# One core, attention and routed experts: heads of the first sequence scaled on GpSimd, 32-bit counts in the searches, and new places for every step

## The chip, the core and the metric

The kernel runs on one core of a Trainium2 chip. The metric is device time in microseconds (us), the median of several executions. TensorE does the matmuls (PE in the profile; PEld is its weight load, which runs beside matmuls), VectorE is DVE, ScalarE is ACT, GpSimd is POOL and SyncE is SP. All work together through semaphores, each in the order in which its instructions are written.

## The reference

`x` has 16 sequences of 256 tokens of 256 channels, all in 32-bit floats.

```
shift = silu(t) @ W_ada.T + b_ada
h = layernorm(x) * g + b + shift
q, k, v = split(h @ Wqkv.T)                 # 16 heads of 64 channels
q, k = layernorm of each head (gain, bias)
x = x + concat(softmax(q k^T / 8) v) @ Wout.T
tok = x.reshape(4096, 256)
gate = softmax(tok @ Wgate.T)               # 8 experts
vals, idx = top_k(gate.T, 512)              # each expert takes its 512 best tokens
g = layernorm(tok[idx])
y = (gelu(g @ fc1.T + b1) @ fc2.T + b2) * vals
tok[idx] += y                               # a token may be taken by several experts
```

## The kernel before

**Attention.** Each sequence is two tiles of 128 tokens. `First` normalises the tokens, transposes them and adds the shift. A `Group` is one of six blocks of 512 columns of the qkv product on one token tile: groups 0 and 1 are q, 2 and 3 are k, 4 and 5 are v. Its matmul (L611) puts 128x512 numbers into PSUM under the tag "mm", which has three buffers. For v, ACT copies them out (L620). For q and k the mean has been taken out of the weights beforehand (`center`, L531 to L533), so that a head's norm needs the squares (ACT, L624), their sum (DVE, L628 and L632), the power -1/2 (POOL, L82), the multiplication (`scale`, L644), four transposes on PE (L653), and an eviction with gain and bias (ACT, L665). `scale` reads PSUM on DVE, unless `keep` has had ACT copy the block to SBUF (L606); then it runs on POOL. In the kernel before only the last sequence has places for `keep`.

A `Quad` is four heads. Scores (L686) are matmuls on half the rows of the array, maxima are on DVE (L693), exponentials on ACT (L702), normalising on POOL (L713), transposes on PE (L722) with copies on DVE or ACT (L730, L732), and the product with v (L740) is on half the columns. `Tail` projects (L764), adds the residual, normalises for the experts and computes gate logits (L797, a 32-bit product of eight columns).

**Routing.** A first routing covers the first 15 sequences' 30 tiles; a second covers all 32 tiles and leaves out what the first has taken. Each picks 256 tokens for every expert by a search over the bits of the threshold: 30 steps, from bit 29 down. A step compares all gates with the candidate and sums the hits of each partition (DVE, L881, into `cnt`), adds these over the 16 partitions of each expert by a matmul with a block matrix, and decides the bit. In the first search (`count_over`) the count comes with a constant taken off, so that its sign decides:

```
nc.tensor.matmul(self.pc, ones[:1, :P], less, start=True, stop=False)
nc.tensor.matmul(self.pc, twice, self.cnt, start=False, stop=True)
```

These are L911 and L912, both in bf16. Meanwhile `either` computes both candidates of the next step (L918, two instructions), and `decide` picks one by a maximum and a minimum (L927). The second search has one count matmul in a step (`count`, L888, with `block`), then `drop` (L893) and `step` (L900).

**Experts.** A job is one expert in one routing: 16 jobs. Onehots (L1031) and their product (L1040) turn places into a list of tokens; `take` makes indices and weights; `gather` fetches the rows by two indirect DMAs from POOL's queue (L1059); transposes (L1068) and an eviction (L1075) follow, then `up` (L1087), gelu (L1094), `down` (L1103), `finish` (L1109, L1110), and `scatter` (L1113), which adds the rows to the output by an indirect DMA from POOL, one for each half of 128 tokens.

**Order.** The order of the instructions is written out by hand. Each step of the attention, of the first routing and of the first jobs has a place number: `STEADY` for a sequence, shifted by its number times `PERIOD`, with `START` in its stead for the first sequences and `END` for the last, and tables for gates, search, lists, `UP` and `DOWN`. `at` collects steps with their places, and all are issued in the order of the numbers. The first search is thus mixed with the attention of the last sequence. The later jobs come from a loop of 16 slots for each job, in which the list and gather of the next job stand at slot 5 and its transposes at slot 14; the second search's steps are dealt out over the slots. Job 0's scatters have places, in the table `DOWN`:

```
at(DOWN[i][1:], partial(jobs[0].scatter, i))
```

**Loads.** SP loads the first sequence, qkv groups 4, 0 and 2 and, each some time ahead, the sequences from the third on. ACT's queue loads the second sequence, groups 1, 3 and 5 and the output weights `wo`, at one place (`LOADS`).

Of the kernel before, what the change touches and what calls it, by code (L numbers as in the profile page):

```python
# [43 lines left out]
def kernel(  # L44
# [35 lines left out]
    def rsqrt(dst, src):  # L80
# [14 lines left out]
    twice = const.tile([P, P], BF16, name="twice")  # L95
    nc.gpsimd.tensor_scalar(twice, block, 2.0, None, ALU.mult)
    less = const.tile([1, 1], BF16, name="less")
    nc.gpsimd.memset(less, -2.0 * (CAP // 2 - 1))
# [30 lines left out]
    nc.gpsimd.memset(gate_of, -1.0)  # L129
    high = const.tile([P, 1], I32, name="high")  # L130
# [9 lines left out]
    PERIOD = 55.238  # L140
    STEADY = dict(
        first=((-88.131, -77.795, -66.865), (-86.413, -85.278, -65.341), (-64.291, -63.624)),
        group={
            (0, 0): (-49.424, -47.476, -46.806, -45.766, -41.767, -39.325, -32.822),
            (0, 1): (-38.888, -36.940, -36.270, -35.230, -33.490, -28.967, -28.300),
            (1, 0): (-19.721, -16.746, -15.194, -14.154, -10.700, -4.932, -1.947),
            (1, 1): (-21.934, -19.241, -18.571, -17.531, -15.791, -5.369, -4.702),
            (2, 0): (-37.170, -35.222, -34.552, -33.512, -31.772, -26.157, -20.051),
            (2, 1): (-27.875, -25.927, -25.257, -24.217, -21.020, -13.051, -9.617),
            (3, 0): (-2.777, -0.829, 1.424, 2.464, 6.338, 15.371, 16.143),  # L150
            (3, 1): (-4.495, -2.547, -1.877, -0.837, 4.102, 8.406, 9.073),
            (4, 0): (-52.511, -43.423),
            (4, 1): (-31.559, -29.611),
            (5, 0): (-16.692, -14.744),
            (5, 1): (-8.179, -6.231),
        },
        quad={
            (0, 0): (0.000, 6.254, 13.508),
            (0, 0, 0): (2.224, 4.501, 6.524, 8.843, 9.510),
            (0, 0, 1): (2.821, 3.601, 7.430, 9.280, 9.947),  # L160
            (0, 1): (-1.059, 4.018, 13.509),
            (0, 1, 0): (0.230, 1.010, 4.288, 7.969, 10.110),
            (0, 1, 1): (0.827, 1.910, 5.194, 7.532, 8.362),
            (1, 0): (11.585, 16.798, 31.441),
            (1, 0, 0): (14.068, 14.848, 17.068, 25.834, 28.523),
            (1, 0, 1): (12.874, 13.654, 17.974, 23.242, 26.227),
            (1, 1): (12.644, 23.095, 31.442),
            (1, 1, 0): (16.201, 20.616, 24.292, 26.708, 27.923),
            (1, 1, 1): (14.665, 21.516, 23.386, 25.397, 27.748),
            (2, 0): (29.518, 34.134, 56.102),  # L170
            (2, 0, 0): (30.807, 31.587, 35.310, 37.672, 38.339),
            (2, 0, 1): (31.404, 32.487, 34.404, 37.235, 37.902),
            (2, 1): (30.577, 35.467, 56.103),
            (2, 1, 0): (32.598, 33.387, 39.367, 46.622, 49.992),
            (2, 1, 1): (32.001, 34.287, 36.216, 38.109, 39.092),
            (3, 0): (40.264, 45.901, 64.955),
            (3, 0, 0): (43.941, 44.721, 46.171, 48.777, 50.676),
            (3, 0, 1): (41.553, 42.333, 47.077, 49.432, 51.346),
            (3, 1): (41.323, 50.592, 64.956),
            (3, 1, 0): (43.014, 43.794, 51.768, 60.225, 60.892),  # L180
            (3, 1, 1): (42.417, 47.782, 50.862, 59.788, 60.639),
        },
        out=(15.601, 33.534, 58.656, 67.053),
        tail=((75.024, 80.051, 81.151, 92.875, 82.383, 82.831, 90.365, 92.705), (97.967, 101.653, 107.912, 115.175, 104.452, 104.900, 115.900, 117.411)),
# [3 lines left out]
            first=((-139.487, -139.084, -130.002), (-134.729, -123.135, -95.026), (-71.635, -61.204)),  # L188
            group={
                (0, 0): (-59.500, -57.180, -53.990, -41.905, -41.892, -31.199, -19.864),  # L190
                (0, 1): (-56.514, -46.937, -42.187, -36.541, -32.975, -14.723, -12.430),
                (1, 0): (-11.345, -10.160, -10.123, -9.363, -7.717, 16.862, 17.870),
                (1, 1): (-17.061, -12.458, -10.932, -9.433, -9.429, -7.544, -7.063),
                (2, 0): (-47.944, -39.268, -37.967, -29.426, -29.083, -19.329, -15.473),
                (2, 1): (-36.593, -35.280, -31.121, -27.896, -26.496, -20.716, -17.116),
                (3, 0): (-0.195, 1.354, 5.032, 6.866, 7.484, 18.359, 20.756),
                (3, 1): (-7.052, -4.047, -4.021, -2.780, 5.168, 9.583, 16.657),
                (4, 0): (-61.161, -56.511),
                (4, 1): (-24.033, -19.174),
                (5, 0): (8.030, 14.550),  # L200
                (5, 1): (-0.065, 4.397),
            },
            quad={
                (0, 0): (-9.254, 22.590, 42.649),
                (0, 0, 0): (-4.098, 3.192, 35.521, 40.175, 42.160),
                (0, 0, 1): (-7.788, -2.839, 22.830, 27.700, 30.119),
                (0, 1): (-10.825, 1.530, 42.650),
                (0, 1, 0): (-9.045, -8.059, 15.256, 16.378, 17.222),
                (0, 1, 1): (-6.921, -0.152, 15.562, 17.096, 23.635),
                (1, 0): (0.126, 14.031, 62.413),  # L210
                (1, 0, 0): (5.581, 9.438, 28.540, 45.916, 48.521),
                (1, 0, 1): (6.615, 11.701, 34.709, 42.123, 45.511),
                (1, 1): (6.647, 32.947, 62.414),
                (1, 1, 0): (12.684, 22.346, 38.667, 41.778, 42.977),
                (1, 1, 1): (16.709, 24.888, 35.995, 40.496, 41.536),
                (2, 0): (36.613, 44.084, 79.640),
                (2, 0, 0): (38.678, 40.096, 53.301, 75.810, 75.857),
                (2, 0, 1): (37.844, 41.179, 46.653, 73.800, 78.092),
                (2, 1): (31.788, 44.810, 79.641),
                (2, 1, 0): (35.309, 35.316, 47.104, 63.762, 75.398),  # L220
                (2, 1, 1): (35.999, 36.383, 45.887, 51.730, 53.463),
                (3, 0): (57.532, 66.273, 80.859),
                (3, 0, 0): (62.041, 62.092, 75.830, 76.948, 78.262),
                (3, 0, 1): (58.897, 62.045, 71.274, 78.272, 80.335),
                (3, 1): (42.288, 56.582, 80.861),
                (3, 1, 0): (53.169, 56.538, 74.699, 79.614, 79.641),
                (3, 1, 1): (55.287, 56.039, 56.589, 75.724, 78.348),
            },
            out=(52.169, 77.187, 79.720, 81.968),
            tail=((83.431, 83.938, 98.840, 128.374, 103.780, 103.911, 108.593, 110.466), (101.110, 104.350, 128.872, 145.215, 106.950, 107.929, 158.941, 161.116)),  # L230
        ),
        1: dict(
            first=((-46.775, -2.928, 1.521), (-17.063, -5.314, 0.982), (15.343, 17.672)),
            group={
                (0, 0): (18.719, 22.736, 28.212, 28.786, 33.289, 38.005, 45.577),
                (0, 1): (21.654, 25.091, 29.577, 30.657, 37.616, 45.616, 50.362),
                (1, 0): (56.965, 58.830, 59.835, 62.211, 62.315, 70.246, 74.608),
                (1, 1): (56.747, 57.357, 58.840, 58.862, 61.374, 62.457, 62.468),
                (2, 0): (40.127, 40.864, 42.252, 42.262, 45.473, 48.208, 52.717),
                (2, 1): (40.977, 41.918, 42.391, 45.462, 46.160, 49.170, 52.410),  # L240
                (3, 0): (74.826, 75.081, 75.503, 78.958, 80.988, 81.454, 84.690),
                (3, 1): (72.447, 74.612, 74.727, 79.840, 80.430, 81.825, 83.328),
                (4, 0): (36.938, 40.518),
                (4, 1): (52.802, 53.597),
                (5, 0): (63.613, 73.243),
                (5, 1): (30.152, 33.881),
            },
            quad={
                (0, 0): (80.434, 81.692, 98.968),
                (0, 0, 0): (80.662, 81.021, 85.076, 94.133, 94.171),  # L250
                (0, 0, 1): (80.458, 80.463, 87.029, 93.291, 94.064),
                (0, 1): (58.862, 78.602, 98.969),
                (0, 1, 0): (66.341, 68.024, 80.857, 85.468, 86.358),
                (0, 1, 1): (68.231, 73.899, 80.721, 81.679, 85.268),
                (1, 0): (80.676, 90.848, 105.478),
                (1, 0, 0): (81.477, 86.038, 92.163, 96.097, 96.147),
                (1, 0, 1): (82.096, 83.656, 93.097, 94.720, 94.811),
                (1, 1): (88.704, 93.176, 105.479),
# [1067 lines left out]
```

## Time and profile before

| | |
|---|---|
| median of 3 executions | 1194.63 us (1194.6 to 1195.56) |
| the profiled execution | 1194.45 us |
| its span | 1192.6 us |
| mean granted clock of TensorE | 0.992 |
| PE busy | 1162.9 us, 98% |
| PEld busy | 817.1 us, 69% |
| DVE busy | 760.9 us, 64% |
| ACT busy | 624.5 us, 52% |
| POOL busy | 590.7 us, 50% |

A group of instructions in the profile shows line, engine, operation, output and input tiles with their shapes and their number, then busy time in all, mean ns of one, and the engine's idle time just before them with what ended it. A wait shows the waiting instruction, what it waited for, and the total in us, how often, and the longest. The granted clock is the share of full speed that the throttle allowed. Line numbers are those of the kernel before.

### The profile page before, as it was taken

The page shows a single profiled execution, that of the slowest core. Times are in us where ns is not written, and L with a number is a line of the kernel's source. Part 1 is how long each engine was busy: PE and PEld are TensorE (multiplying, and loading weights), DVE is VectorE, ACT ScalarE, POOL GpSimd, SP SyncE. Part 2 cuts the span into 40 slices and gives each one's busy share as a digit, 9 for nine tenths or more (in the row PEclk, how much of TensorE's full clock was granted, in tenths as well). Part 3 has the DMA queues.
Part 4 walks back from the last instruction along what each step waited for, and adds up shares of the span by engine and source line. Part 5 has one row for each costly group of instructions (what it writes and reads, how often), then busy time and mean ns, then how long its engine had stood idle before and what let it go on. Part 6 is the DMA issues. An engine that isn't in the chain of part 4 may idle for free. (4 is left out here: it accounts for less than half of the span.)

```text
span 1192.6 us, 19612 instructions
## 1 busy us (share of the span) xinstructions
PE 1162.9 (98%) x6814; PEld 817.1 (69%) x6814; DVE 760.9 (64%) x2274; ACT 624.5 (52%) x1701; POOL 590.7 (50%) x820
## 2 busy tenths in 40 slices
PE   7999999999999999999999999999998989999996
PEld 3566666666676666666666666667755878888885
DVE  7665576666566666666666666565588557865541
ACT  2765655565565656565656566556574422333331
POOL 4665455545555555555554555464674233333332
PEclk9999999999999999999999999999999999999999
DMA  5000000000000000000000000000200446666661
GB/s 187 1 1 5 14 18 19 10 18 10 19 23 5 23 10 19 10 23 6 23 10 28 9 11 14 14 19 19 85 9 1 168 129 186 186 186 185 183 185 22
DMA packets 46738, 62.40 MB, mean 52 GB/s; under 512 B 3888, under 2 KB 39984, under 8 KB 46640
## 3 DMA queue, kind: packets, MB, share of 16 engines
q1 hardware_dynamic: 37680, 49.82, 12.3%
q0 software_dynamic: 6144, 8.39, 3.8%
q10 hardware_dynamic: 2816, 2.95, 0.7%
q8 instruction: 54, 0.88, 0.3%
q14 instruction: 44, 0.36, 0.1%
HBM read 48.56 MB, written 12.58 MB: 51 GB/s over the span
## 5 line engine op out<-in xcount | busy, mean ns | idle before, releaser
L611 PE MATMUL pm<-wq,hT 128*128 128x512 f32 x768 | 365.3, 606 | 2.2 <-ACT qT L665 0.9
L713 POOL TENSOR_SCALAR pr<-pr,sums 128x256 f32<-128x256 f32 x512 | 236.8, 481 | 208.9 <-DVE sums L709 162.2
L82 POOL TENSOR_TENSOR ss<-ss,neghalf 128x8 f32<-128x8 f32 x128 | 211.5, 1653 | 189.8 <-DVE ss L632 185.4
L702 ACT ACTIVATE pr<-sc,nmax 128x256 f32<-128x256 f32 x512 | 236.1, 474 | 116.1 <-DVE nmax L693 111.1
L611 PEld LDWEIGHTS pm<-wq,hT 128*128 128x128 f32 x768 | 134.9, 192 | 126.3 <-issue 112.2
L693 DVE TENSOR_REDUCE nmax<-sc 128x2 f32<-128x512 f32 x256 | 166.5, 683 | 38.3 <-PE sc L686 38.1
L628 DVE TENSOR_REDUCE ss<-sq 128x8 f32<-128x512 f32 x128 | 87.3, 682 | 112.0 <-ACT sq L624 111.5
L722 PEld LDWEIGHTS pp<-ident,pr 128*128 128x128 f32 x1024 | 119.1, 142 | 43.6 <-POOL pr L713 20.3
L722 PE MATMUL pp<-ident,pr 128*128 128x128 f32 x1024 | 139.2, 273 | 0.2
L624 ACT ACTIVATE sq<-pm 128x512 f32<-128x512 f32 x128 | 76.7, 600 | 113.6 <-PE pm L611 107.1
L686 PE MATMUL sc<-kT,qT 64*128 64x256 f32 x1024 | 129.2, 390 | 0.0
L740 PE MATMUL po<-prT,v 128*64 128x256 f32 x1024 | 126.7, 389 | 0.0
L686 PEld LDWEIGHTS sc<-kT,qT 64*128 64x128 f32 x1024 | 93.2, 186 | 40.6 <-issue 30.4
L1103 PE MATMUL py<-w,hid 128*128 128x256 f32 x512 | 118.8, 385 | 0.0
L1087 PE MATMUL ph<-xT,w 128*128 128x256 f32 x512 | 118.4, 384 | 0.0
L764 PE MATMUL pw<-wo,oT 128*128 128x256 f32 x512 | 118.0, 384 | 0.0
L1113 POOL DMA_INDIRECT out<-y,idx x32 | 51.6, 1611 | 123.9 <-DVE y L1110 72.9
L764 PEld LDWEIGHTS pw<-wo,oT 128*128 128x128 f32 x512 | 96.8, 192 | 18.9 <-issue 6.5
L1094 ACT ACTIVATE hid<-ph,vec 128x256 f32<-128x256 f32 x128 | 60.3, 473 | 85.5 <-PE ph L1087 73.4
L1103 PEld LDWEIGHTS py<-w,hid 128*128 128x128 f32 x512 | 95.8, 192 | 13.4
L702 ACT ACTIVATION_READ_ACCUMULATOR pr<-sc,nmax 128x1 f32 x512 | 104.9, 205 | 0.0
L1087 PEld LDWEIGHTS ph<-xT,w 128*128 128x128 f32 x512 | 95.3, 191 | 13.4
(129 smaller groups left out, 1290.7 us busy)
## 6 DMA issues: line engine op xcount, KB each, us to landing
w<-in_fc2T SPq DMA_DIRECT2D x16, 1024.0 KB, 5.6
w<-in_fc1T SPq DMA_DIRECT2D x16, 1024.0 KB, 8.0
out<-tok SPq DMA_DIRECT2D x32, 128.0 KB, 1.7
xn_dram<-tn SPq DMA_DIRECT2D x32, 128.0 KB, 1.7
xs<-in_x SPq DMA_DIRECT2D x15, 256.0 KB, 2.7
b<-in_b2s SPq DMA_DIRECT2D x16, 128.0 KB, 8.2
wq<-in_wqkvT SPq DMA_DIRECT2D x3, 512.0 KB, 6.6
wq<-in_wqkvT ACTq DMA_DIRECT2D x3, 512.0 KB, 6.6
```

Source lines behind the costliest of these rows:

```text
L82: nc.gpsimd.tensor_tensor(dst, src, neghalf[:, : src.shape[1]], ALU.pow)
L611: nc.tensor.matmul(self.pm, hTs[self.b][:, c, bass.ts(self.t, P)], wq[:, c, bass.ts(self.g, GW)], start=(c == 0), stop=(c == DC - 1),)
L628: nc.vector.tensor_reduce(self.ss[:, 0, :], self.sq.rearrange("p (h d) -> p h d", d=HD), AX.X, ALU.add,)
L686: nc.tensor.matmul(self.sc[i, j][:, t, :], qTs[self.b][rows, hp, bass.ts(t, P)], kTs[self.b][rows, hp, :], start=True, stop=True,)
L693: nc.vector.tensor_reduce(self.nmax[i, j], self.sc[i, j], AX.X, ALU.max, negate=True)
L702: nc.scalar.activation(self.pr[i, j][:, t, :], self.sc[i, j][:, t, :], AF.Exp, bias=self.nmax[i, j][:, t : t + 1], scale=1.0, accum_out=se ...
L713: nc.gpsimd.tensor_scalar(self.pr[i, j][:, t, :], self.pr[i, j][:, t, :], self.sums[i][:, 1, j, t : t + 1], 1.0, ALU.mult, ALU.mult,)
L722: nc.tensor.transpose(self.pp[i, j][:, c, bass.ts(t, P)], self.pr[i, j][:, t, bass.ts(c, P)], ident,)
L740: nc.tensor.matmul(self.po[j * HD : (j + 1) * HD, i, :], vs[self.b][:, c, bass.ts(4 * self.d + 2 * i + j, HD)], self.prT[i, j][:, c, :], s ...
L764: nc.tensor.matmul(self.pw, oTs[self.b][:, hp, bass.ts(self.t, P)], wo[:, hp, :], start=(hp == 0), stop=(hp == HP - 1),)
L1087: nc.tensor.matmul(self.ph[f], self.w1[:, c, bass.ts(f, P)], self.xT[:, c, :], start=(c == 0), stop=(c == DC - 1),)
L1103: nc.tensor.matmul(self.py[i], self.hid[:, f, bass.ts(i, P)], self.w2[:, f, :], start=(f == 0), stop=(f == FC - 1),)
```

## The change

- **Counts in 32 bits.** `cnt` becomes a 32-bit float, `blockf` is a 32-bit copy of `block`, and `twice` is a 32-bit float. The second search counts with `blockf`. In the first, the comparison starts its sum on each partition at -(256-1)/16, and the one-row matmul with the constant goes.
- **Candidates from a table.** `change` holds, for each bit, the two words with which the candidate is XORed; `either` becomes one instruction. Five small DVE instructions fill the table at place 4.5 periods, and POOL prepares its exponents.
- **First sequence.** Its eight q and k groups get a place for `keep`: ACT copies them out of PSUM, and POOL scales them.
- **Loads.** ACT's queue takes the second sequence and qkv groups 5, 1 and 3 at one place, and the third sequence, `wo`, the fourth and the fifth at a second one. SP loads the sequences from the sixth on.
- **Job 0's scatters.** Only the half that ends first has a place; the other is issued behind job 2's gather.
- **New places** for every step, and `PERIOD` 55.497 in place of 55.238.

```diff
+    blockf = const.tile([P, P], F32, name="blockf")
+    nc.gpsimd.tensor_copy(blockf, block)
+    twice = const.tile([P, P], F32, name="twice")
     nc.gpsimd.tensor_scalar(twice, block, 2.0, None, ALU.mult)
-    less = const.tile([1, 1], BF16, name="less")
-    nc.gpsimd.memset(less, -2.0 * (CAP // 2 - 1))
...
+    change = const.tile([P, 30, 2], I32, name="change")
+    powers = const.tile([P, 31], I32, name="powers")
+    nc.gpsimd.iota(powers, pattern=[[1, 31]], base=126, channel_multiplier=0)
+
+    def fill_change():
+        nc.vector.tensor_scalar(powers, powers, 23, None, ALU.logical_shift_left)
+        nc.vector.tensor_copy(change[:, :, 0], powers[:, :30].bitcast(F32))
+        nc.vector.tensor_tensor(
+            change[:, :, 1], powers[:, :30].bitcast(F32), powers[:, 1:].bitcast(F32), ALU.add
+        )
+        for k in range(2):
+            nc.vector.memset(change[:, 0, k : k + 1], k)
...
-    PERIOD = 55.238
+    PERIOD = 55.497
...
     START = {
         0: dict(
...
-                (0, 0): (-59.500, -57.180, -53.990, -41.905, -41.892, -31.199, -19.864),
+                (0, 0): (-73.721, -55.814, -49.484, -45.811, -35.989, -25.285, -20.864, -40.370),
...
         def later_loads():
             load_x(1, nc.scalar)
-            for g in (1, 3, 5):
+            for g in (5, 1, 3):
                 load_wq(g, nc.scalar)
+
+        def last_loads():
+            load_x(2, nc.scalar)
             nc.scalar.dma_start(wo, woutT.rearrange("(h p) d -> p h d", p=P))
+            for b in (3, 4):
+                load_x(b, nc.scalar)
...
-            def compare(self, n):
+            def compare(self, n, begin=0.0):
                 reach = bit.tile([P, 2 * P], BF16, tag="reach", name="reach")
-                self.cnt = bit.tile([P, 1], BF16, tag="cnt", name="cnt")
+                self.cnt = bit.tile([P, 1], F32, tag="cnt", name="cnt")
                 nc.vector.tensor_scalar(
-                    reach, self.gT, self.cand.bitcast(F32), None, ALU.is_ge, ALU.add,
+                    reach, self.gT, self.cand.bitcast(F32), begin or None, ALU.is_ge, ALU.add,
                     accum_out=self.cnt,
                 )
...
-                nc.tensor.matmul(self.pc, block, self.cnt, start=True, stop=True)
+                nc.tensor.matmul(self.pc, blockf, self.cnt, start=True, stop=True)
...
+            def compare_less(self, n):
+
+                self.compare(n, -(CAPL - 1) / 16)
+
             def count_over(self, n):
...
-                nc.tensor.matmul(self.pc, ones[:1, :P], less, start=True, stop=False)
-                nc.tensor.matmul(self.pc, twice, self.cnt, start=False, stop=True)
+                nc.tensor.matmul(self.pc, twice, self.cnt, start=True, stop=True)
 
             def either(self, n):
-                self.next = []
-                for name, op in (("keep", ALU.bitwise_or), ("drop", ALU.bitwise_xor)):
-                    new = bit.tile([P, 1], I32, tag=name, name=name)
-                    nc.vector.tensor_scalar(
-                        new, self.cand, 0 if name == "keep" else 1 << n, (1 << n) >> 1,
-                        op, ALU.bitwise_or,
-                    )
-                    self.next.append(new)
+                self.next = bit.tile([P, 2], I32, tag="next", name="next")
+                nc.vector.tensor_tensor(
+                    self.next, self.cand.to_broadcast([P, 2]), change[:, n, :], ALU.bitwise_xor
+                )
...
-            if b > 1:
+            if b > 4:
                 at([min(its["first"][t][0] for t in range(TB)) - 20.0], partial(load_x, b))
...
+        at([4.5 * PERIOD], fill_change)
...
-            at(DOWN[i][1:], partial(jobs[0].scatter, i))
+        by_end = sorted(range(KL), key=lambda i: DOWN[i])
+        at(DOWN[by_end[0]][1:], partial(jobs[0].scatter, by_end[0]))
...
                     new.gather()
+                    if k == 1:
+                        jobs[0].scatter(by_end[1])
```

The other lines of the diff are the tables of places.

## The prediction

> **What bounds the kernel now.** The profiled execution took 1194.45 us, its span 1192.6, so 1.85 us lie outside; the median, 1194.63, is 0.18 us above it. The sum below goes by the profiled time. I read the page's first part (PE busy 1162.9 us, 98%), then the windows by stage, PE's waits, the groups, and the timeline where the windows show holes.
>
> ```profile
> 0.00:20.00 20.00, 13.47 (x31) 6.68 (x32) 13.82 (x34) 4.80 (x8) 9.26 (x24) 1.00 0.82 278
> 20.00:40.00 20.00, 17.55 (x64) 8.52 (x62) 16.23 (x36) 11.43 (x27) 9.06 (x7) 0.91 0.01 2
> 255.20:310.50 55.30, 55.30 (x320) 36.78 (x319) 35.80 (x83) 32.60 (x95) 29.78 (x45) 1.00 0.05 15
> 850.00:900.00 50.00, 47.23 (x276) 30.05 (x274) 39.73 (x164) 29.46 (x82) 31.37 (x45) 1.00 0.17 56
> 900.00:950.00 50.00, 45.30 (x293) 35.02 (x290) 36.22 (x176) 17.94 (x42) 18.39 (x30) 0.93 0.21 70
> 950.00:1000.00 50.00, 46.55 (x300) 39.47 (x299) 30.83 (x161) 15.71 (x32) 17.47 (x18) 0.97 0.56 164
> ```
>
> Columns: stretch, length, busy time of PE, PEld, DVE, ACT, POOL, then granted clock and DMA. A steady sequence (third line) has PE busy throughout: only PE work counts there. Holes lie at the start, around the first search (867 to 909 us) and until job 2's gather (965 us). The clock column counts too: 0.91 over 20 us is 3.6 us at half rate, 0.93 and 0.97 over 50 us are 7 and 3.
>
> ```profile
> PE pa L499 <- ACT sT L494: 5.1, 1, 5.1
> PE pc L912 <- DVE reach L881: 4.0, 14, 0.5
> PE px L1068 <- DMA xg<-xn_dram,idx: 3.8, 3, 2.6
> POOL out L1113 <- DMA out<-y,idx: 6.9, 1, 6.9
> ```
>
> The first wait is before the first matmul and is not touched. The other three are what the edits aim at.
>
> ```profile
> L644 DVE TENSOR_TENSOR qk<-pm,ss 128x512 f32<-128x512 f32 x120 | 81.3, 678 | 9.3 <-POOL ss L82 9.0
> L644 POOL TENSOR_TENSOR qk<-qk,ss 128x512 f32<-128x512 f32 x8 | 8.4, 1065 | 0.1
> L82 POOL TENSOR_TENSOR ss<-ss,neghalf 128x8 f32<-128x8 f32 x128 | 211.5, 1653 | 189.8 <-DVE ss L632 185.4
> L606 ACT COPY qk<-pm 128x512 f32<-128x512 f32 x8 | 4.6, 594 | 0.2 <-PE pq L653 0.2
> L911 PE MATMUL pc<-less,ones 1*128 1x1 bf16 x30 | 5.2, 172 | 0.0
> L912 PE MATMUL pc<-cnt,twice 128*128 128x1 bf16 x30 | 5.1, 170 | 4.3 <-DVE reach L881 4.0 <-ACT prT L732 0.3
> ```
>
> The eight POOL scales are the last sequence's; they price the first sequence's.
>
> **Part 1, the start: -4.0 us.** PE's spacing here against its steady spacing (429 ns per pass of L611, 109 per transpose) gives 5.6 us lost between 17 and 27 us: waits of 1.2, 1.8 and 1.1 at 17.6, 20.2 and 22.4, the rest in the half-rate stretch 23.4 to 26.9. Each wait is for a DVE scale or ACT's eviction behind it: a pm buffer is held through square 0.60, reduce 0.68+0.18, power 1.65 and scale 0.68. With the ACT copy it is free after square and copy, 1.2 us, and DVE loses 8 x 0.68 = 5.4 us of work. ACT gains 8 x 0.59 = 4.7 us; it was 11.43 of 20 us busy. POOL gains 8 x 1.065 = 8.5 us and serves a tile every 2.72 us. Walking the new order with these durations, PE is dense from about 18 us (L611 resumes at 18.05, now 18.84), and the first scores come at 30.6 with ten projection tiles done, now 31.9 with eight. That is 1.3 + 2 x 1.72 = 4.7 ahead; I take off 0.7 for short waits (0.3 each) behind ACT's added DMA issues: xs2, wo, xs3 and xs4 now go through ACT's queue, later; SP is passed by no load that anyone waits for then. The added constants on POOL delay its first power by some 0.2 us, inside this. Bounds: -5.5 (all of the loss gone) to +4.3 (last rival).
>
> A page would give less: the Trainium skill, "GPSIMD Engine Reference", section 4.1, "Engine selection", advises VectorE for elementwise work because GpSimd is about 2 times slower for two-input operations. The rows say 1065 against 678 ns, a factor of 1.57; by the page's factor it would be an estimated 1356 ns, and eight scales would cost 2.3 us more on POOL.
>
> **Part 2, the first search: +1.9 us.** A step's chain now is compare to accumulated 0.485, 0.06 to PE, the count, 0.2 to decide, decide to next compare 0.32: 1.06 us. Where PE has work between two counts (14 of 29 gaps), that work plus 0.33 for two counts sets the step; the sum of the larger ones over the gaps is 41.8 us, the trace shows 41.1 from 867.9 to 909.1. The matmul of one row goes, but its issue lies in the wait for the other, so I give nothing for it alone. The two either-instructions (146 and 144 ns) become one on DVE, off the chain. The 32-bit product runs two passes of 112 ns (the shortest 32-bit product, L797, issues so), hence one more pass in the chain: 1.17 per step, or PE's work plus 0.224. Over the new gaps that is 40.1; I take 40.5. But between the counts stand 25.36 us of other PE work, now 27.85; the rest moved ahead of the search, where PE was full. PE's loss goes from 41.1 - 27.85 = 13.25 to 15.1. Bounds: -5 (the pass hidden and the one-row matmul's change of tile worth 0.2 per step) to +4. The table's five small DVE instructions at 4.5 periods (some 0.15 each, from L918's rows) lie under steady DVE slack, 35.8 of 55.3 busy; uncovered, 0.8.
>
> **Part 3, the second search: +3.4 us.** Its 30 counts cost PE 0.111 each in bf16; between full-rate matmuls the second pass costs 30 x 0.112. No chain hides it: PE is full there. Bounds 2.5 to 6 (an uncovered weight load: 98 ns for bf16, 191 for the 32-bit L797).
>
> **Part 4, new places: +1.4 and +0.7.** Entering and leaving a block of row- or column-tiled matmuls costs about 0.35 us by the spacing (95 and 104 ns in, 97 and 58 out). Counting blocks in both orders, the new one has about four more: 1.4. Steady work of PE is otherwise the same. The smallest slack there falls for the copies of the transposed exponentials, from 3.8 to 2.5 us, against 0.85 needed, and rises for q and k from 8.2 to 10.1: no stall. For stalls in sequences 12 to 15 I allow 0.7 (0 to 2).
>
> **Part 5, until job 2's gather: -6.6 us.** The timeline:
>
> ```profile
> 957.61 1.57 POOL L1113 DMA_INDIRECT out<-y,idx  x1 [6.87 <-DMA out<-y,idx]
> 960.71 1.05 POOL L1059 DMA_INDIRECT xg<-xn_dram,idx  x1
> 962.06 0.99 POOL L1059 DMA_INDIRECT xg<-xn_dram,idx  x1 [0.30 <-issue]
> 963.77 0.30 PE L1068 MATMUL px<-ident,xg 128*128 128x128 f32 x1 [2.57 <-DMA xg<-xn_dram,idx]
> ```
>
> Job 0's second scatter waits 6.87 us for the first one to land; the gather, whose indices were ready at 953.3, queues behind it. PE loses 2.7, then 1.1 and 1.5 around it: 5.3. With that scatter behind the gather, the gather issues after the POOL casts at about 955, some 9 us of PE work ahead of its use. What then waits behind the scatter are job 1's scatters, due later. Further 1.3: the list's onehots and first transposes are spread so that 909 to 930, which now loses 8 us, ends a little better. Bounds -7.5 to -2. The clock adds to both: each half-rate stretch of 3.4 us costs up to 1.7.
>
> On the clock, the Trainium skill, "TensorE: Matmul & The Clock Gate", Part 1, says that the activity window runs free of the kernel. If so, which of the four half-rate stretches go is not decided by the order alone; no run here shows it yet.
>
> **Sum:** -4.0 + 1.9 + 3.4 + 1.4 + 0.7 - 6.6 = -3.2. From 1194.45 this gives 1191.25; on the median's scale 1191.4.
>
> **Rivals.** (a) The search gains instead: the product's second pass is hidden by the next load and the one-row matmul's tile change was in the chain; -5 in place of +1.9, 1184.5 to 1187. For: PEld L911 waits 10.0 us on issue. Against: the chain of 1.06 explains the steps. 0.10. (b) The gather's wait stays, because the casts or the landing come last now: +5.3, so +2.1, 1196.7. Against: 9 us of cover. 0.12. (c) The edits do less than they say, with a period 0.26 us longer as its constant is, over 11 steady sequences: +2.9, 1194.3. Against: the same PE work. 0.13. (d) Slower: POOL becomes the bound at the start. In its first 55 us it would have 21.7 of powers and scales, 32 normalisations of 0.48 (15.4) and the next sequence's eight powers (13.2): 50.3. If four scales fall behind what PE waits for, 4 x 1.065 = 4.3 late in place of 4.0 early: +5.1, 1199.7. It decides as soon as the start is not 0.8 us better than now. 0.15.
>
> **How the numbers follow.** The forecast has 0.50, its own range 1188.5 to 1194. A measurement here tells 0.2%, 2.4 us, from no change. Faster by more: 0.10 + 0.40 of the forecast's + 0.02 of (c) = 0.52; slower by more: (d) 0.15, half of (b) 0.06, 0.04 of (c), 0.01 = 0.26; the rest 0.22. The range 1187 to 1198 leaves out most of (a) and of (d).
>
> **What would show it.** Right: 20 to 40 us with PE above 19 us at a clock near 1.00; eight more POOL scales of about 1065 ns; the first to last count of the search 40 to 41 us; px waiting on its gather under 0.5 us; counts twice as many as before, their loads near 191 ns; steady stretches of 55.3 with PE full. Wrong: PE waiting on POOL's qk in the first 50 us (d); a search under 38 us (a); a px wait still over 2 us (b); PE holes between 60 and 850 us (c).

## The result and the profile after

The changed kernel is slower. Its median is 1198.73 us over 19 executions, against 1194.89 for 19 of the kernel before: a ratio of 1.0039, 95% interval 1.003 to 1.0048. The forecast was 1191.4 with a range to 1198.0, so the sign was wrong and the time lies just outside the range. Three executions of later runs lie far above all others (2076 us in one run, 1500 and 3650 in another), and the medians below leave them out.

The executions of the changed kernel lie in three groups, near 1196, 1198.5 and 1200.8. The profiled one took 1200.69 (span 1199.0), so its trace shows about 2 us more than the median. Its windows, columns as before:

```profile
20.00:40.00 20.00, 17.47 (x75) 9.21 (x74) 14.96 (x35) 14.02 (x28) 15.95 (x14) 1.00 0.30 93
850.00:900.00 50.00, 45.63 (x252) 30.13 (x252) 36.68 (x130) 26.77 (x76) 27.59 (x44) 0.96 0.16 56
900.00:950.00 50.00, 40.33 (x264) 29.86 (x261) 33.81 (x155) 17.38 (x41) 15.53 (x24) 0.91 0.20 67
950.00:1000.00 50.00, 50.00 (x329) 44.44 (x327) 32.20 (x166) 15.85 (x31) 16.75 (x17) 1.00 0.58 166
```

The last line shows the hole at job 2's gather gone. The two lines above it show PE busy 6.6 us less than before over 850 to 950 us, with the clock lower. The first line, the start, has a full clock and yet no more busy time (PE does 75 matmuls in it, 64 before). The waits and groups:

```profile
PE pc L935 <- DVE reach L901: 7.2, 11, 0.9
PE pls L1058 <- POOL oh L1049: 2.6, 5, 0.7
PE pm L631 <- DVE wq L553: 2.0, 1, 2.0
PE px L1086 <- DMA xg<-xn_dram,idx: 1.1, 2, 0.6
```

```profile
L664 POOL TENSOR_TENSOR qk<-qk,ss 128x512 f32<-128x512 f32 x16 | 16.6, 1041 | 0.6
L935 PE MATMUL pc<-cnt,twice 128*128 128x1 f32 x60 | 11.4, 259 | 7.4 <-DVE reach L901 7.2
L908 PEld LDWEIGHTS pc<-cnt,blockf 128*128 128x128 f32 x60 | 11.4, 190 | 1.5
```

The changed kernel's lines lie 15 to 20 further down: L901 is the comparison, L935 the first search's count, L664 the scale. The wait for the comparison grew from 4.0 to 7.2 us, the counts are twice as many, and PE waits 2.0 us for centred weights at the start. From the first to the last count the first search takes 47.7 us in this execution; it took 41.1. One step in which nothing else holds PE, before and after (rows picked from the timeline: start, duration, instruction):

```profile
905.89 0.16 PE L912 MATMUL pc<-cnt,twice 128*128 128x1 bf16 x1 [0.23 <-DVE reach L881]
906.40 0.48 DVE L881 TENSOR_SCALAR_CACHE_REDUCE reach<-gT,cand 128x256 bf16<-128x256 f32 x1
906.58 0.10 PEld L912 LDWEIGHTS <-twice 128*128 128x128 bf16 x1
906.95 0.16 PE L912 MATMUL pc<-cnt,twice 128*128 128x1 bf16 x1 [0.29 <-ACT prT L732]
```

```profile
912.03 0.30 PEld L935 LDWEIGHTS pc<-cnt,twice 128*128 128x128 f32 x2 [0.64 <-DVE reach L901]
912.03 0.38 PE L935 MATMUL pc<-cnt,twice 128*128 128x1 f32 x2 [0.40 <-DVE reach L901]
912.77 0.48 DVE L901 TENSOR_SCALAR_CACHE_REDUCE reach<-gT,cand 128x256 bf16<-128x256 f32 x1
913.31 0.38 PE L935 MATMUL pc<-cnt,twice 128*128 128x1 f32 x2
```

From count to count it was 1.06 us and is 1.28. The stages:

| stage | before | after |
|---|---|---|
| first count at | 867.96 us | 868.17 us |
| first search | 41.1 us | 47.7 us |
| last count to job 2's first up matmul | 59.5 us | 55.6 us |
| from there to the last matmul | 213.8 us | 216.8 us |

### The profile page after: what moved, and what is told of

It reads as the page before. It is cut to its first block, busy times and chain, and to the rows that moved or that the text cites. A ratio compares the mean times of both kernels' runs of the same rounds, so it can differ in the third digit from the quotient of the medians.

```text
span 1199.0 us, 19707 instructions
## 1 busy us (share of the span) xinstructions
PE 1166.0 (97%) x6844; PEld 822.3 (69%) x6844; DVE 758.5 (63%) x2241; ACT 628.0 (52%) x1709; POOL 597.4 (50%) x829
## 5 line engine op out<-in xcount | busy, mean ns | idle before, releaser
L631 PE MATMUL pm<-wq,hT 128*128 128x512 f32 x768 | 360.0, 598 | 2.7 <-DVE wq L553 2.0
L752 ACT COPY prT<-pp 128x512 f32<-128x512 f32 x144 | 82.0, 588 | 86.2 <-PE pp L742 86.2
L750 DVE COPY prT<-pp 128x512 f32<-128x512 f32 x112 | 76.4, 684 | 48.3 <-PE pp L742 48.1
```

The lines of the kernel that those rows point to most:

```text
L631: nc.tensor.matmul(self.pm, hTs[self.b][:, c, bass.ts(self.t, P)], wq[:, c, bass.ts(self.g, GW)], start=(c == 0), stop=(c == DC - 1),)
```

## The experiments

Theory P: the 32-bit product lengthens each step of the search, and the longer idle lets the clock fall in it. Its rivals put the loss on the new order, or on the removed one-row matmul. All runs below are compared with the kernel before on the same chip; its median was 1194.65 to 1195.23 in the three sets.

**The first search back in bf16** (with its `cnt`, and the comparison without its start value), everything else as changed:

```diff
-    twice = const.tile([P, P], F32, name="twice")
+    twice = const.tile([P, P], BF16, name="twice")
...
+    less = const.tile([1, 1], BF16, name="less")
+    nc.gpsimd.memset(less, -2.0 * (CAP // 2 - 1))
...
+                nc.tensor.matmul(self.pc, ones[:1, :P], less, start=True, stop=False)
-                nc.tensor.matmul(self.pc, twice, self.cnt, start=True, stop=True)
+                nc.tensor.matmul(self.pc, twice, self.cnt, start=False, stop=True)
```

> The changed kernel with the first search's counts put back to the two bf16 matmuls (one-row constant and count); the second search stays in 32 bits, all places stay. Theory P (the 32-bit product lengthens every step: the traces have 1.28 us for a step without PE work between, against 1.06 before, and the longer idle lets the clock fall twice or three times inside the search): the search falls from 47.8 us to about 40.3 (sum over the gaps of the larger of 1.06 and PE's work plus 0.33), no half-rate stretch inside it, the whole 5.5 to 7.5 us faster than the changed kernel, so about 1191 to 1193. Rival O (the new order fills the gaps badly, whatever the type): the search stays above 45 us, the gain under 2 us.

1193.19 us, ratio 0.9992 (0.9983 to 1.0001), so 5.5 us below the changed kernel. The search took 40.0 us. The stretch from 868 to 909 us, first in the changed kernel, then in this one:

```profile
868.00:909.00 41.00, 34.84 (x192) 22.46 (x191) 31.14 (x117) 22.80 (x68) 21.73 (x34) 0.88 0.00 1
```

```profile
868.00:909.00 41.00, 34.22 (x233) 22.19 (x233) 35.78 (x143) 27.21 (x79) 25.41 (x42) 1.00 0.00 1
```

The new order is not at fault for the search: with bf16 counts it gives one 1.1 us shorter than before, at a clock of 1.00.

**Both searches in bf16**: also `block` in place of `blockf`, and `cnt` in bf16 throughout.

> The changed kernel with the counts of both searches put back to bf16 (the first with the one-row matmul). Against the run with only the first search put back, theory P expects another 3.4 us less (30 second passes of 0.112 us in the second search, where PE is full): 1188 to 1190. The rival, that the second search's passes hide in weight loads, expects under 1 us between the two.

1189.68 us, ratio 0.9963 (0.9949 to 0.9976), 3.5 us below the run before it. From job 2's up to the end it takes 213.7 us instead of 216.8. The passes of the second search do not hide. Together the 32-bit counts cost 9.0 us; the rest of the change gains about 5.

**The one-row matmul put back** ahead of the 32-bit product, the comparison without its start value:

```diff
...
+                nc.tensor.matmul(self.pc, ones[:1, :P], less, start=True, stop=False)
-                nc.tensor.matmul(self.pc, twice, self.cnt, start=True, stop=True)
+                nc.tensor.matmul(self.pc, twice, self.cnt, start=False, stop=True)
```

> The changed kernel with the one-row bf16 matmul put back ahead of the 32-bit product in the first search, and the comparison without its start value. Theory P: the pass in the chain remains, so the step stays at 1.28 us and the time within 1.5 us of the changed kernel. Rival C (the one-row matmul, issued early in the wait, kept the clock up): the half-rate stretches inside the search go, about 3.5 us faster than the changed kernel at an unchanged step of 1.28.

1202.37 us, ratio 1.0064 (1.005 to 1.0078). Rival C falls: the time rose by 3.6 us. The shortest step stays at 1.28 us, longer ones rise by about 0.1, and in the profiled execution, 4.0 us above the median, the search takes 52.1 us with 17 us at half rate, from 891.1 to 894.5 and from 901.3 to 915.0. Theory P's bound of 1.5 us was too narrow as well.

**Matmuls put into the search's waits**, for the clock:

```diff
-                self.pc = ps.tile([P, 1], F32, tag="mm", bufs=3, name="pc")
+                pc = ps.tile([P, GW], F32, tag="mm", bufs=3, name="pc")
+                if n in (25, 23, 21, 20, 19, 16, 14, 13, 12, 11, 8, 6, 4, 3, 2, 1, 0):
+                    for _ in range(2):
+                        nc.tensor.matmul(pc[:, 256:], block, ones, start=True, stop=True)
+                self.pc = pc[:, :1]
                 nc.tensor.matmul(self.pc, twice, self.cnt, start=True, stop=True)
```

> The changed kernel with two bf16 matmuls of 256 columns (0.107 us each, result unused) ahead of the count in the 17 of the first search's steps that have at most 0.9 us of PE work since the count before. They lie in time in which PE waits for the comparison. Theory P with the clock as its second half: no half-rate stretch in the search, the search at about 43 us (sum of the larger of 1.28 and PE's work plus 0.31), 3 to 4 us faster than the changed kernel. If the clock costs nothing here or is not moved by this: no gain, 0 to 2 us slower.

1197.10 us, ratio 1.0027 (1.0018 to 1.0037): 1.6 us below the changed kernel's median, and 4.4 below its profiled execution (1196.25 in this run's profile). The same stretch, in this run:

```profile
868.00:909.00 41.00, 36.47 (x247) 24.89 (x248) 34.31 (x133) 25.97 (x76) 23.73 (x39) 1.00 0.00 1
```

PE has more to do, and the clock holds at 1.00. The search takes 43.3 us, where 43.0 follow from 1.28 us for a step, or PE's work plus 0.31. So the chain alone explains 43.3, and the clock the rest: 4.4 us in the changed kernel's profile and less at its median, since the number of half-rate stretches differs between executions. (In the run with the scatter put back, below, the same search has one, and takes 44.9.) The other runs agree: in the eight profiles whose first search counts in bf16 no half-rate stretch lies between its first and last count, and in the five with 32-bit counts and no added matmuls at least one does.

**The kernel before with only its first search in 32 bits**:

```diff
-                nc.tensor.matmul(self.pc, ones[:1, :P], less, start=True, stop=False)
-                nc.tensor.matmul(self.pc, twice, self.cnt, start=False, stop=True)
+                nc.tensor.matmul(self.pc, twice, self.cnt, start=True, stop=True)
...
-            at(p, *(partial(f, n) for f in (first.compare, first.count_over, first.either, first.decide)))
+            at(p, *(partial(f, n) for f in (first.compare_less, first.count_over, first.either, first.decide)))
```

(`twice` and the first search's `cnt` become 32-bit floats, and `compare_less` starts the sum at the constant, as in the changed kernel.)

> The kernel before with the first search alone in 32 bits: one product of the 32-bit count, the constant as the comparison's start value; no table, all places and the second search as before. Theory P: with 1.28 us for a step without PE work and PE's work plus 0.31 otherwise, the sum over this order's 29 gaps is 44.9 us where 41.1 were measured, so +3.8, and up to 3.4 more if the clock falls inside the search: 1198.5 to 1202. Rival O (only the new order made the search long): within 1 us of the kernel before.

1201.04 us, ratio 1.0052 (1.0038 to 1.0067), about 5.8 us slower. The search takes 48.8 us, with half rate from 883.0 to 893.2. The same part costs the same in the other order.

**The scatter alone**, in the kernel before:

```diff
-            at(DOWN[i][1:], partial(jobs[0].scatter, i))
+        by_end = sorted(range(KL), key=lambda i: DOWN[i])
+        at(DOWN[by_end[0]][1:], partial(jobs[0].scatter, by_end[0]))
...
                     new.gather()
+                    if k == 1:
+                        jobs[0].scatter(by_end[1])
```

> The kernel before with only job 0's later scatter moved behind job 2's gather. Theory S (the gather was queued on POOL behind a scatter that waited for the landing of the one before): px's wait goes, job 2's first up matmul comes 5 us earlier, 1189 to 1190.5. Rival W (another wait takes its place on POOL, the casts or the landing): the gather moves by under 2 us, 1193 or more.

1189.67 us, ratio 0.9954 (0.9941 to 0.9966). From job 1's to job 2's first up matmul it takes 15.5 us instead of 20.8. This one edit makes the kernel before as fast as the changed kernel with all counts in bf16 (1189.68): the new order, the table, the loads and the scales on POOL together gain nothing beyond it.

**The scatter put back**, in the changed kernel (the reverse edit):

> The changed kernel with both of job 0's scatters back at their places, ahead of job 2's gather. Theory S: 4 to 5.5 us slower than the changed kernel, 1202.5 to 1204, with px waiting on the gather again. Rival W: no change, under 1.5 us.

1198.71 us, ratio 1.0035 (1.0021 to 1.0048): no change. Theory S holds in the old order and not in the new one. The issues around it, in the kernel before and then here (of the two weight loads of a job, the first):

```profile
947.96 0.38 SPq L1003 DMA_DIRECT2D w<-in_fc2T  x1
949.07 1.67 POOL L1113 DMA_INDIRECT out<-y,idx  x1 [11.43 <-DVE y L1110]
957.61 1.57 POOL L1113 DMA_INDIRECT out<-y,idx  x1 [6.87 <-DMA out<-y,idx]
```

```profile
951.66 1.67 POOL L1131 DMA_INDIRECT out<-y,idx  x1 [12.76 <-DVE y L1128]
954.00 0.38 SPq L1021 DMA_DIRECT2D w<-in_fc2T  x1
956.49 1.57 POOL L1131 DMA_INDIRECT out<-y,idx  x1 [3.16 <-DMA out<-y,idx]
```

Before, the first scatter is issued just behind the loads of a job's 2 MB of weights, and the second can go 8.5 us later. In the new order it is issued 2.3 us ahead of them, and the second goes after 4.8 us, before the list at 958 us that the gather needs. That the loads slow the scatter is read from this order of issues; no run moved the loads alone.

**The first sequence's scale on DVE**, in the changed kernel:

```diff
-                engine, src = nc.gpsimd, self.qk
+                engine, src = nc.vector if self.b == 0 else nc.gpsimd, self.qk
```

> The changed kernel with the first sequence's eight scales on DVE instead of POOL, still from the copy in SBUF and at the same places. Theory D (DVE, which also takes the mean out of the weights, sets the start; PE's longest wait there is 2.0 us for it): 8 x 0.68 us more work on DVE, 1 to 3 us slower than the changed kernel. Rival G (POOL with power and scale, 2.7 us for a tile, sets the start): 1 to 2 us faster.

1206.17 us, ratio 1.0085 (1.0068 to 1.0102): 7.4 us slower than the changed kernel, where theory D gave 1 to 3. Rival G falls. The first count comes 5.5 us later; the profile also has two more half-rate stretches than the changed kernel's, at 30.8 us. PE's wait for the centred weights grows:

```profile
PE pm L631 <- DVE wq L553: 7.2, 1, 7.2
```

DVE sets the start here, and POOL's scales are a help. The trace of the changed kernel shows one reason why they help less than forecast (rows picked out):

```profile
19.22 1.04 POOL L664 TENSOR_TENSOR qk<-qk,ss 128x512 f32<-128x512 f32 x1
19.56 0.73 DVE L652 TENSOR_SCALAR ss<-ss 128x8 f32<-128x8 f32 x1
24.30 2.04 POOL L664 TENSOR_TENSOR qk<-qk,ss 128x512 f32<-128x512 f32 x2
25.50 0.86 DVE L652 TENSOR_SCALAR ss<-ss 128x8 f32<-128x8 f32 x1
28.16 1.04 POOL L664 TENSOR_TENSOR qk<-qk,ss 128x512 f32<-128x512 f32 x1
28.54 0.68 DVE L552 TENSOR_SCALAR ws<-ws 128x8 f32<-128x8 f32 x1
```

Three DVE instructions that take 0.17 us elsewhere end 0.02 to 0.03 us after the POOL scale that runs over them: 1.76 us of DVE time lost. The Trainium skill, "SBUF — State Buffer", "Who interferes with whom", has a rule for it: DVE and GpSimd share a port pair as an exclusive lock, which `tensor_scalar` can take in a two-port mode, though not in the form that also writes out its accumulator. So the next run used that form.

**Two of the small instructions in the accumulating form**, on the kernel with both searches in bf16. (The two tiles get the factor 1/64 from ACT's square. A third edit, to the weights' mean, fell on another instruction than the long one.)

```diff
+                self.plain = self.b == 0 and (self.g, self.t) in ((0, 0), (2, 1))
...
+                if self.plain:
+                    total = stat.tile([P, 1], F32, tag="total", name="total")
+                    nc.vector.tensor_scalar(
+                        self.ss[:, 0, :], self.ss[:, 0, :], EPS, None, ALU.add, ALU.add,
+                        accum_out=total,
+                    )
+                    return
                 nc.vector.tensor_scalar(
                     self.ss[:, 0, :], self.ss[:, 0, :], 1.0 / HD, EPS, ALU.mult, ALU.add
```

> The changed kernel with all counts in bf16, and at the start the three small DVE instructions that took 0.73, 0.86 and 0.68 us in place of 0.17 (each ended 0.02 to 0.04 us after a POOL scale that ran over it) written in the form that also sums into an accumulator. Theory L (POOL's scale of two SBUF operands holds something that the plain form of these DVE instructions needs, and the comparison's form does not): they take about 0.17 plus 0.085 for reading the accumulator each, PE gets its group 1 us earlier, 0.5 to 1.5 us faster than the run with both searches in bf16. Rival: they are long for another reason and stay above 0.5 us; no change in time.

1188.47 us, ratio 0.9951 (0.9933 to 0.9969), 1.2 us below the run that it edits (which ran on another chip, where the kernel before is 0.5 us faster).

```profile
19.58 0.16 DVE L665 TENSOR_SCALAR_CACHE_REDUCE ss<-ss 128x8 f32<-128x8 f32 x1
24.97 0.16 DVE L665 TENSOR_SCALAR_CACHE_REDUCE ss<-ss 128x8 f32<-128x8 f32 x1
27.53 1.53 DVE L561 TENSOR_TENSOR wq<-wq,ws 128x512 f32<-128x512 f32 x1
```

Both take 0.16 us now, as theory L and the page have it. The third POOL scale, at 27.48, now falls on a DVE instruction with two operands in SBUF, which takes 1.53 us instead of 0.69. The profile of the unedited run has a half-rate stretch at 30.7 us, this one has none. The run with only the first search in bf16 has the same start and none either; against it the first count comes 0.9 us earlier (867.4 instead of 868.4), which is what the edit is worth at the same clock.

**Five onehots of job 0's list on POOL in place of ten**, on the kernel with both searches in bf16:

```diff
-                engine = nc.gpsimd if a is jobs[0] and k in (2, 5) else nc.vector
+                engine = nc.gpsimd if a is jobs[0] and k == 2 else nc.vector
```

> The changed kernel with all counts in bf16, and five instead of ten of job 0's onehots on POOL (0.66 us each there, 0.18 on DVE). In the changed kernel's trace POOL ends its ten 6.6 us after the search's places are known, DVE its twenty about 4, and PE's list waits 2.6 us for POOL. Expected: the list ends 1 to 1.5 us earlier, the time 1 to 3 us lower (more if the half-rate stretch behind it goes). If DVE with 25 of them becomes the later one: no change.

1187.74 us, ratio 0.9955 (0.9938 to 0.9972), 1.9 us below the run that it edits, as expected. The list ends 12.0 us after the last count instead of 14.6, and PE's wait for POOL there is gone. About 1 us of this is the clock: the profile of the unedited run has a half-rate stretch in the list, this one has none, and where both profiles have one (the next run) the list ends after 12.9.

**Both edits:**

> The two edits together on the changed kernel with all counts in bf16: 1186.5 to 1189.5 if both work and add.

1187.54 us, ratio 0.994 (0.9922 to 0.9959): 2.1 us below the run that they edit, where the two apart gave 1.2 and 1.9.

**The kernel before with the scatter and the five onehots:**

> The kernel before with job 0's later scatter behind job 2's gather and five of job 0's onehots on POOL in place of ten: 1 to 2.5 us below the run with the scatter alone, 1187 to 1189.

1187.01 us, ratio 0.994 (0.9923 to 0.9957). Two small edits of the old kernel do as well as the new order with bf16 counts and the two edits above. Both beat the two kernels that were compared.

## Why the prediction was wrong

**The first search (Part 2) is the step that failed.** It gave 40.5 us; the profiled execution has 47.7, and 44.9 with a single half-rate stretch. Its model of the step was right in kind; three of its terms were wrong.

- The step's chain was put at 1.17 us, with one more pass at the issue spacing of the short 32-bit product (112 ns). It is 1.28. Comparison to count is 0.54 us in both kernels, but count to next comparison grew from 0.51 to 0.74, twice the price of that pass. The other half lies at the weight loads. In the step shown the weights of the bf16 count were loaded ahead, during the wait (906.58 for the count at 906.95). In 26 of the 30 32-bit counts the first load starts with the count or 0.03 us ahead of it, the second 0.08 us or more behind the count's start, and the second pass, at full rate, 0.03 us behind that load. In the other four the first load ran 0.1 us or more ahead: the passes start 0.03 us apart, and the one of these steps that PE's other work does not lengthen (909.58) takes 1.18 us, as forecast. That the second pass waits for its load is read from this order; no run changed the loads alone. The prediction priced an uncovered load for the second search only.
- Steps with PE work between cost that work plus 0.31, not plus 0.224. Together with the chain this gives 43.0 us at a full clock, so by the prediction's own 25.36 us of other work PE's loss in the search rises from 13.25 to 17.6 us: +4.4, where the prediction had +1.9.
- The clock was only given a width, and none in this place. At 1.00 the search took 43.3 (fillers); half-rate stretches add the rest. The searches in bf16 also leave PE idle and keep a clock of 1.00 until the last count; what tips the balance is not settled, since the one-row matmul made it worse and the wider matmuls cured it.

"New order" and "new type" were taken together there. Apart, the order with bf16 counts is good for 40.0 us, and the type costs 5.5 us at the median.

**The second search (Part 3)** was right: +3.4 forecast, 3.5 in the medians, 3.1 in the stage.

**The start (Part 1)** failed too. From its first matmul to 60 us, against the spacing of the same pairs of matmuls in steady sequences, PE loses 8.0 us instead of 9.6: a gain of 1.6, not 4.0. That gain goes with the clock. The kernel before has a half-rate stretch at 23.4 us in its profile, the changed one has none; the kernel before with its first search in 32 bits, whose start is the old one, has none either, and loses 7.9. Where the profiles have a stretch, the old start loses 9.6 to 9.9 and the new one 8.4 to 9.0. So at the same clock the new start gains between nothing and about 1 us. The walk took each engine's durations as independent of the others; POOL's scales cost DVE 1.76 us, and the first scores come at 34.3, not 30.6. Two of the three waits taken away gave 0.9 back, so this is only part of what is missing. The rival that POOL itself becomes the bound was wrong.

**The work moved ahead of the search (Parts 2 and 4)** was put at 2.5 + 1.4 = 3.9 us, with 0.7 for stalls. Between the two profiles without a half-rate stretch at the start, the first count comes at 868.2 in the new order and at 865.9 in the old: 2.2 us. So that the first count came near the 868.6 that the sum implies is luck: the start gained less than forecast, the moved work cost less, and the half-rate stretch fell in one profile and not in the other.

**Until job 2 (Part 5)** the gain is 3.9 us, not 6.6, and part of it may be the clock's: three half-rate stretches lie in this stage before, one after. The old order with the scatter alone takes 54.4 us for it, the changed kernel 55.6. The wait at the gather is worth 5.1 to 5.3, as forecast, but the cause was only right for the old order: in the new one the move of the scatter is worth nothing. The further 1.3 at the list did not come: ten onehots on POOL still hold it up, as the run with five shows.

**Steady sequences** were right: PE stays full in them. The factor of GpSimd against DVE was 1041 to 681 ns, so the row of the kernel before was a better guide than the factor of 2 of the page that the prediction cites.

The rivals: (a), a search that gains, has the opposite sign of what happened; (b) and (c) did not come; (d) had the right sign and the wrong place, so that its 1199.7 lies near the time measured is chance. No rival had the count's type as the loss, although Part 2's upper bound of +4 lies near the +4.4 that it costs at a full clock.

## What to carry to other kernels

On a chain that runs through PE, price a matmul from the moment its input is ready to the moment its result is used, with the weight loads that cannot run ahead, and not by its issue spacing alone; thirty steps turn 0.1 us into 3. A wait that is lengthened on PE is priced with the clock that it may cost, and such idle time can be worth filling. Before a gain between two profiles is put down to an edit, look at where each has its half-rate stretches. Before two edits aimed at the same wait are counted, try each alone: here either of them removed it, and the second was worth nothing.

## What the runs showed of the hardware

- A plain `tensor_scalar` on DVE over SBUF waits until a GpSimd `tensor_tensor` with two SBUF operands has ended (0.73, 0.86 and 0.68 us for 0.17); the accumulating form does not (0.16). A DVE `tensor_tensor` with two SBUF operands took 1.53 us beside such a scale, 0.69 otherwise.
- A 32-bit product of one column runs as two passes with a weight load for each (60 loads for 30 counts). As a chain's link it costs 0.22 us more than a bf16 one, and 0.12 where the first load has run ahead.
- Half-rate stretches are multiples of 3.4 us, and their number and place differ between runs with the same start: at 30.7 us in one profile and absent in another of the same order. The three groups of times, about 2.4 us apart, go with that (mean clock 0.996, 0.993 and 0.990 to 0.992); that the clock makes all of the spacing was not shown.
